# Layer 0 reordered: router ahead of the other transposes, convolution behind the expert tiles, lag terms by outer products

## The chip, the cores and the metric

The kernel runs on one core of a Trainium2 chip. All of its numbers are float32. The metric is the device time of one execution in microseconds (us). The core has five engines that run their own in-order queues side by side: PE (TensorE, matmuls and transposes, with its weight loads shown apart as PEld), DVE (VectorE), ACT (ScalarE), POOL (GpSimd) and SP (SyncE, which here only issues DMAs). POOL issues the indirect DMAs, those whose rows are found by a list of indices. Engines wait for one another by semaphores.

## The reference, cut to what matters

The program is four layers over x of 16 sequences of 256 tokens of 128 features. Only layer 0 is touched by the change:

```python
xn = layernorm(x)                                  # no scale, no shift
x  = x + L0_attn(xn) + L0_ffn(xn)

def L0_attn(x):                                    # a state space layer, 64 states for each of 128 channels
    u  = layernorm(x) * ln_gamma + ln_beta
    dt = exp(log_dt)
    dA = exp(-exp(log_A) * dt[:, None]); dB = B_param * dt[:, None]
    # for each step t:  h = dA*h + dB*u[..., None];  y[t] = einsum('dn,bdn->bd', C_param, h) + D_param*u
    return x + y @ W_out.T + b_out

def L0_ffn(x):                                     # 8 experts, the two best of each token, and a shared expert
    xn = layernorm(x) * ln_scale + ln_bias
    probs = softmax(xn @ gate_w.T);  top 2, scaled to sum to 1 -> w
    out = swiglu(x, sWg, sWu, sWd)
    for e in range(8):
        out = out + w[:, e:e+1] * swiglu(x, Wg[e], Wu[e], Wd[e])
    return out                                     # swiglu(x, g, u, d) = (silu(x@g) * (x@u)) @ d
```

The recurrence is linear, so y is a causal convolution of u along the sequence. Its weight at lag l, in channel d, is the sum over the 64 states n of C[d,n] * B[d,n] * dt[d] * exp(-exp(log_A[d,n]) * dt[d] * l), and D[d] is added at lag 0.

The other layers (attention over 16 heads and a gated network; a window of 3 and a ternary network; attention and a coupling network) follow in the same program.

## The kernel before, in words

The 4096 tokens lie in 8 blocks X[0] to X[7] of 512 tokens; a block is 128 partitions by 4 groups by 128 features. Blocks 0 to 3 are half 0, blocks 4 to 7 half 1.

`prepare(hf)` (L163) does, for one half: mean and variance of X (`stats`, L115), r = 1/std (`inv_std`, L107), xn (`normalise`, L122), its transposes xT (L173), the sum X + xn on POOL (L175), statistics of xn once more, z = xn normalised a second time, z's transposes, the router's scale and shift on DVE (rT, L186), the logits (lg, L189), and `route` (L209). `route` picks the two best experts of each token and gives each (token, expert) a slot in a list sorted by expert, in tiles of 256 slots that each belong to one expert (23 tiles a half, 46 in all). For that it counts, for every token and expert, the tokens ahead of it: within a group of 128 tokens by a product with a triangular matrix, and over the groups ahead by 15 products with a matrix of ones into the same bank (pos, L243 to L245).

`scatter` (L294) writes the rows xn to their slots in DRAM (XS), by 32 indirect DMAs a half. XS is filled with zeros first, by four DMAs from a tile of 128 x 2944 zeros (L154).

The convolution needs the lag weights. `lag_rates`, `lag_terms` and `lags_done` (L315 to L334) work them out state by state: for each of 64 states an Exp of 128 x 256 on ACT (dec) and a multiply-add on DVE into kern; kern goes to DRAM (kd). `convolved` (L196) makes u from z (gamma, beta on DVE), turns it round in time by a product with a reversed identity (ru) and puts it into U. `toeplitz(g)` (L339) loads, for four channels, 128 overlapping windows of kd as a matrix of 128 x 4 x 256 (toe, 512 KB), and `conv(g)` (L345) multiplies it with U (cv) and copies the result to Y; g runs to 32. `mixed(i)` (L439) transposes Y and adds its product with W_out and the bias to X.

The tile loop (L480 to L499) works on tile k: `fetch_weights` (the expert's weights, POOL, four tiles ahead), `fetch_slots` (256 rows xs of XS, SP, three ahead), `turn_slots` (two transposes, xsT), `up_slots` (sg, su, silu and product hs) and `down_slots` (sy, its copy ys, and a store to YS). From tile 6 on one conv(g) goes with each tile. From tile 29 on, `fetch_outputs` gathers the rows of half 0 back from YS (yk, POOL) and `combine` adds them, weighted, to X. Behind the loop follow mixed for half 0, then half 1's gathers beside mixed for half 1, then half 1's combines.

What sets the order: inside `tc.manual_schedule` (L467) each engine issues the instructions of the region in the order in which they are written. Outside it, and for how the instructions of the region fall among the others, a planner that works with costs of its own decides; of two ready instructions it takes the one that was written first. A queue doesn't overtake: an instruction that waits holds back what is behind it on its engine, SP's and POOL's DMA issues included.

## Time and profile before

| | |
|---|---|
| median of 14 runs | 1717.78 us (1710.58 to 1729.92) |
| the profiled execution: its own time | 1724.39 us |
| its span, first to last instruction | 1722.4 us |
| mean granted clock of PE | 0.909 |
| layer 0 up to the first matmul of layer 1 (pq) | 525.3 us |
| of that: first transposes of a tile (xsT) at | 210.3 us |
| last sy of the last tile ends at | 446.3 us |

The page shows for each engine a row of 40 digits: the busy tenths of 40 equal slices of the span. Rows of stages give the stretch, its length, then the busy time of PE, PEld, DVE, ACT and POOL with the number of instructions, the granted clock, the share of the DMA engines and GB/s. Rows of the timeline give start, duration, engine, line, operation, written and read tiles, how many were merged, and in brackets the idle time of the engine before it and what ended it. "issue" there means that nothing in the profile explains the wait; "remote" means a semaphore whose sender isn't seen. Rows of the chain give start, duration, engine and tile. A matmul of float32 stands as two passes, so 8 products are x16.

### The profile page before, as it was taken

To read this page: it belongs to the slowest core of one execution; us is meant where nothing else is said; L and a number is where in the kernel's file an instruction comes from. 1 tells how busy PE (TensorE), PEld (TensorE's weight loads), DVE (VectorE), ACT (ScalarE), POOL (GpSimd) and SP (SyncE) were. 2 spreads that over 40 slices of the span, in tenths; PEclk is the share of its full clock that TensorE was granted. 3 is DMA by queue.
4 is the path that set the end of the run, shared out by engine and by line. 5 is a ranking of instruction groups with operands and counts; after the bars stand their busy time and mean duration, and the time that the engine had idled before them with its cause. 6 is when DMAs were issued, how large, how long until landed. Compare 5 with 4: busy or idle time off the path is not lost.

```text
span 1722.4 us, 28078 instructions
## 1 busy us (share of the span) xinstructions
PE 1485.5 (86%) x11820; PEld 951.7 (55%) x11820; DVE 747.3 (43%) x1644; ACT 656.9 (38%) x1047; POOL 278.5 (16%) x269
## 2 busy tenths in 40 slices
PE   3646489988827999999999999999989999998998
PEld 2434378887514666666555455555545666664344
DVE  6537122222256555553344333533335655552223
ACT  2336222221104454443224333433334445435543
POOL 1442421145360000000001111111100000000222
PEclk9966799998758899998999999999998999988898
DMA  6120267785130000000000000000000000000000
GB/s 229 37 68 17 76 183 224 223 243 152 45 135 1 2 2 2 2 2 2 1 1 1 1 1 0 0 1 0 0 1 2 2 2 2 2 2 1 0 25 25
DMA packets 60142, 73.78 MB, mean 43 GB/s; under 512 B 5233, under 2 KB 53490, under 8 KB 59378
## 3 DMA queue, kind: packets, MB, share of 16 engines
q1 hardware_dynamic: 51376, 43.18, 7.8%
q0 software_dynamic: 7920, 27.08, 5.6%
q8 instruction: 94, 1.54, 0.4%
q10 hardware_dynamic: 722, 1.73, 0.3%
q14 instruction: 30, 0.25, 0.0%
HBM read 53.42 MB, written 18.55 MB: 42 GB/s over the span
## 4 chain that ended last, share of the span: by engine, by line
PE 72%; DVE 9%; ACT 7%; DMA 6%; issue 4%; another core or an unknown queue 2%; POOL 1%; SPq 0%; DVEq 0%; ACTq 0%; POOLq 0%
PE h L105 13%; PE se L105 8%; PE sc L105 7%; PE po L105 7%; PE c L105 5%; DMA xs<-XS 5%; PE av L105 4%; ACT E L688 4%; DVE M L646 3%; PE mT L661 2%; PE pq L105 2%; PE cv L105 2%; PE sg L105 2%; PE pv L105 2%
## 5 line engine op out<-in xcount | busy, mean ns | idle before, releaser
L646 DVE TENSOR_REDUCE M<-sc 128x4 f32<-128x1024 f32 (+3 forms) x256 | 196.0, 819 | 113.8 <-PE sc L105 113.8
L105 PE MATMUL h<-h,pk 128*128 128x512 f32 x512 | 221.0, 592 | 0.0
L688 ACT ACTIVATE E<-se 128x1024 f32<-128x1024 f32 (+1 forms) x192 | 158.8, 879 | 107.2 <-PE se L105 107.0
L105 PEld LDWEIGHTS h<-h,pk 128*128 128x128 f32 x512 | 97.3, 190 | 119.0 <-issue 115.3
L105 PE MATMUL sc<-Kp,Qm 32*128 32x192 f32 (+3 forms) x2048 | 136.3, 349 | 21.7 <-ACT E L688 21.5
L105 PE MATMUL se<-Q,Km 32*128 32x256 f32 (+3 forms) x2048 | 131.4, 344 | 13.2 <-DVE M L646 11.6
L105 PEld LDWEIGHTS sc<-Kp,Qm 32*128 32x128 f32 x2048 | 100.3, 198 | 70.1 <-ACT E L688 35.0
L815 POOL TENSOR_TENSOR pr<-q,k 128x512 f32<-128x512 f32 (+2 forms) x24 | 28.4, 1210 | 607.3 <-ACT k L808 429.8
L105 PEld LDWEIGHTS se<-Q,Km 32*128 32x128 f32 x2048 | 94.5, 194 | 51.9 <-issue 44.4
L939 POOL TENSOR_TENSOR xT<-xT,c 128x512 f32<-128x512 f32 x24 | 30.2, 1278 | 442.2 <-DVE c L938 442.2
L865 ACT ACTIVATE h<-h,pk 128x512 f32<-128x512 f32 x64 | 44.0, 687 | 144.3 <-PE h L105 144.2
L875 DVE TENSOR_TENSOR x<-x,po 128x512 f32<-128x512 f32 x8 | 5.5, 688 | 170.4 <-PE po L105 170.4
L133 PE MATMUL xnT<-consts,xn 128*128 128x128 f32 x128 | 28.5, 364 | 59.0 <-DVE xn L124 59.0
L412 DVE TENSOR_TENSOR hs<-hs,su 128x512 f32<-128x512 f32 x46 | 31.6, 688 | 108.7 <-PE su L105 91.3
L105 PE MATMUL av<-E,vals 128*32 128x256 f32 (+3 forms) x2048 | 78.4, 306 | 0.0
L297 POOL DMA_INDIRECT XS<-xn,slots x64 | 63.4, 991 | 63.6 <-DVE te L277 44.4
L381 POOL DMA_INDIRECT we<-in_w0e,rows x46 | 43.9, 954 | 166.5 <-PE sy L105 99.9
L105 PE MATMUL c<-c,pk 128*64 128x512 f32 (+2 forms) x144 | 70.1, 635 | 0.0
L430 POOL DMA_INDIRECT yk<-YS,slots x64 | 60.7, 949 | 33.7 <-issue 15.8
L105 PE MATMUL py<-shared,h 128*128 128x128 f32 x128 | 20.2, 311 | 53.2 <-issue 25.8
L703 ACT COPY cu<-av 128x512 f32<-128x512 f32 x32 | 18.8, 586 | 121.8 <-PE av L105 121.8
L105 PEld LDWEIGHTS cv<-U,toe 128*128 128x128 f32 x512 | 64.1, 197 | 1.9
(227 smaller groups left out, 2630.6 us busy)
## 6 DMA issues: line engine op xcount, KB each, us to landing
toe<-kd SPq DMA_DIRECT2D x32, 512.0 KB
XS<-zero SPq DMA_DIRECT2D x4, 1472.0 KB
xs<-XS SPq DMA_DIRECT2D x46, 128.0 KB
YS<-ys SPq DMA_DIRECT2D x46, 128.0 KB
pk<-in_pk SPq DMA_DIRECT2D x1, 3145.5 KB
x<-in_x SPq DMA_DIRECT2D x8, 256.0 KB
out<-x SPq DMA_DIRECT2D x8, 256.0 KB
XS<-xn,slots POOLq DMA_INDIRECT x64
```

Source lines behind the costliest of these rows:

```text
L105: nc.tensor.matmul(o, l, r, start=start, stop=stop)
L133: nc.tensor.transpose(ps[:, t * P : (t + 1) * P], src[:, t, :], ident)
L297: d = nc.gpsimd.indirect_dma_start(out=XS[hf][:, :], out_offset=at_rows(slots[hf][:, k, n : n + 1]), in_=xn[n // NT][:, n % NT, :], in_off ...
L381: nc.gpsimd.indirect_dma_start(out=w["w"].rearrange("p a b -> p (a b)"), out_offset=None, in_=w0e[:, :], in_offset=at_rows(rows_of[hf][:, ...
L412: nc.vector.tensor_tensor(h, h, pu, ALU.mult)
L430: nc.gpsimd.indirect_dma_start(out=y, out_offset=None, in_=YS[hf][:, :], in_offset=at_rows(slots[hf][:, k, n : n + 1]))
L646: nc.vector.tensor_reduce(dst, src, AX.X, ALU.max, negate=True)
L661: nc.tensor.transpose(ps[:, T, c * P : (c + 1) * P], negm[bl][:, c, T].rearrange("p g j k -> p (g j k)"), ident)
L688: nc.scalar.activation(E[:, 2 * n : 2 * n + 2, :], se[n][:, :, 0 : 2 * wide], AF.Exp, scale=ISQ)
L815: nc.gpsimd.tensor_tensor(pr[:, :, j:], q[:, :, j:], k[:, :, 0 : S - j], ALU.mult)
L865: nc.scalar.activation(hn[:, c, :], ps, AF.Gelu, scale=W2[sn][:, c : c + 1])
L939: nc.gpsimd.tensor_tensor(xT[i], xT[i], cpl, ALU.add)
```

## The change

It rewrites layer 0's order and three of its parts. Nothing behind layer 0 is touched.

- **prepare**: the second normalisation is worked out from the first one's figures (r1 and off), so z comes straight from X, on ACT, without xn and without a second round of statistics. z, the logits and `route` are written ahead of xn, its transposes and xT. rT moves from DVE to ACT, the copy of the logits from ACT to DVE, and X + xn out of it (now `add_norm`, on DVE, between tiles).
- **route**: the 15 products of ones become one, and the sum over the groups ahead becomes a scan on DVE (four doublings).
- **zeros**: one DMA a half, from a tile of 128 x 128 that is read again and again, and only after the last input has landed.
- **lag terms**: exp(rate * l) is split into exp(rate * fine) * exp(rate * coarse) with l = coarse + fine, each 16 values; the sum over states is 128 small products on PE (`lag_sums`), 64 rows by 16 columns, and eight stores to kd. `lag_rates`, `lag_terms`, `lags_done` go.
- **order**: half 0's 32 scatters and the first 15 of half 1's are written ahead of the loop; the other 17 go one at the start of each of the first 17 tiles. Between up_slots and down_slots of every second tile goes one piece of: lag_sums; then for each block add_norm, for half 1 its shared expert, and convolved. The 32 toeplitz and conv steps follow the loop, with half 1's gathers and combines between them; then mixed for all 8 blocks, then the last combines.

```diff
-        zero = wp.tile([P, TILES * SLOTS // 2], F32, tag="zero", name="zero")
+        zero = wp.tile([P, D], F32, tag="zero", name="zero")
...
-            flat = XS[hf].rearrange("(q p n) d -> q p (n d)", q=2, p=P)
-            zeroed.append([nc.sync.dma_start(out=flat[q], in_=zero) for q in range(2)])
+            flat = XS[hf].rearrange("(p n) d -> p n d", p=P)
+            zeroed.append([nc.sync.dma_start(out=flat, in_=zero.unsqueeze(1).to_broadcast([P, TILES * SLOTS // P, D]))])
+            for z in zeroed[hf]:
+                tc.add_manual_dep(z.ins, xin[-1].ins.name, sync, reason="inputs first")
...
             r = inv_std(sp, mv, N, "r0" + tag)
+            nc.vector.tensor_tensor(r1, r, r, ALU.mult)
+            nc.vector.tensor_tensor(r1, r1, mv[:, :, 1], ALU.mult)
+            nc.vector.tensor_scalar(r1, r1, EPS, None, ALU.add)
+            nc.scalar.activation(r1, r1, AF.Sqrt)
+            nc.vector.reciprocal(r1, r1)
+            nc.vector.tensor_tensor(r1, r1, r, ALU.mult)
+            nc.vector.scalar_tensor_tensor(off, mv[:, :, 0], -1.0, r1, ALU.mult, ALU.mult)
...
+                for t in range(NT):
+                    k = n * NT + t
+                    nc.scalar.activation(
+                        z[:, t, :], X[i][:, t, :], AF.Identity, bias=off[:, k : k + 1], scale=r1[:, k : k + 1]
+                    )
+                ps = transpose4(z, f"zT{i}")
+                rT = sp.tile([P, 512], F32, tag="rT", name=f"rT{i}")
+                nc.scalar.activation(rT, ps, AF.Identity, bias=W0["lnb"], scale=W0["lns"])
...
+            route(logits, hf)
             for n, i in enumerate(blocks):
                 normalise(xn[n], X[i], mv, r, n * NT)
                 ps = transpose4(xn[n], f"xnT{i}")
                 nc.scalar.copy(xT[i], ps)
-                nc.gpsimd.tensor_tensor(X[i], X[i], xn[n], ALU.add)
-                stats(sp, xn[n], mv1[:, n * NT : (n + 1) * NT, :], f"st1_{i}")
...
-            mm(pos[:, 0 : N * E], W0["upper"], flat, True, False)
-            for k in range(1, N):
-                mm(pos[:, k * E : N * E], ones2, flat[:, 0 : (N - k) * E], False, k == N - 1)
+            mm(pos[:, 0 : N * E], W0["upper"], flat)
+            mm(pos[:, N * E : 2 * N * E], ones2, flat)
...
+            while k < N:
+                V.tensor_copy(run[1][:, 0:k, :], run[0][:, 0:k, :])
+                V.tensor_tensor(run[1][:, k:N, :], run[0][:, k:N, :], run[0][:, 0 : N - k, :], ALU.add)
+                run.reverse()
+                k *= 2
...
+        def lag_sums(parts):
+            ps = [bank(f"lag{h}") for h in range(2)]
+            for k in range(16):
+                for c in range(4):
+                    for h in range(2):
+                        r = slice(64 * h, 64 * h + 64)
+                        mm(
+                            ps[h][32 * c : 32 * c + 16, 16 * k : 16 * k + 16], parts["coarse"][r, 4 * k + c, :],
+                            parts["fine"][r, 4 * k + c, :],
+                        )
+            for h in range(2):
+                for c in range(4):
+                    r = slice(32 * c, 32 * c + 16)
+                    nc.vector.tensor_copy(kt[r, h], ps[h][r, 0:256].rearrange("p (k b) -> p k b", b=16))
...
+            for h in range(2):
+                for c in range(4):
+                    dst = bass.AP(
+                        tensor=kd.tensor, offset=kd.offset + (64 * h + c) * 384 + P,
+                        ap=[[16, 16], [4 * 384, 16], [1, 16]],
+                    )
+                    nc.sync.dma_start(out=dst, in_=kt[32 * c : 32 * c + 16, h])
...
-        lag_rates()
         xn0, zs0 = prepare(0)
         for n in range(HN):
-            scatter(0, xn0, n)
+            for k in range(2):
+                scatter(0, xn0, n, k)
+        xn1, zs1 = prepare(1)
+        inside = TILES - 6
+        early = 2 * HN - inside
+        second = [(n, k) for n in range(HN) for k in range(2)]
+        for nk in second[:early]:
+            scatter(1, xn1, *nk)
         for i in HALVES[0]:
             shared_expert(i)
-        convolved(0, zs0)
-        xn1, zs1 = prepare(1)
-        for n in range(HN):
-            scatter(1, xn1, n)
-        for s in range(0, 64, 4):
-            lag_terms(range(s, s + 4))
-        lags_done()
-        for i in HALVES[1]:
-            shared_expert(i)
-        convolved(1, zs1)
+        parts = lag_weights()
...
+        between = [lambda: lag_sums(parts)]
+        for i in range(NBLK):
+            between.append(lambda i=i: add_norm(i))
+            if i in HALVES[1]:
+                between.append(lambda i=i: shared_expert(i))
+            between.append(lambda i=i: convolved(i, zs[i]))
...
             for k in range(NJ):
+                if k < inside:
+                    scatter(1, xn1, *second[early + k])
                 if k + 4 < NJ:
                     fetch_weights(k + 4)
...
-                g = k - 6
-                if 0 <= g < 32:
-                    if g + 3 < 32:
-                        toeplitz(g + 3)
-                    conv(g)
+                if between and k % 2 == 0:
+                    between.pop(0)()
                 down_slots(k)
...
+            for g in range(3):
+                toeplitz(g)
+            for g in range(32):
+                if g + 3 < 32:
+                    toeplitz(g + 3)
+                conv(g)
+                if g == 0:
+                    combine(0, HN - 1)
+                if g % 2 == 1 and g // 2 + 4 < HN:
+                    fetch_outputs(1, g // 2 + 4)
+                if g >= 6 and g % 2 == 0 and (g - 6) // 2 < HN:
+                    combine(1, (g - 6) // 2)
+            for i in range(NBLK):
                 mixed(i)
-            for n in range(5):
-                fetch_outputs(1, n)
-            for i in HALVES[1]:
-                mixed(i)
-            for n in range(HN):
-                if n + 5 < HN:
-                    fetch_outputs(1, n + 5)
+            for n in range(13, HN):
                 combine(1, n)
```

## The prediction

> **What bounds the kernel now.** I read the page, then busy time by stage, then the timeline where engines stand still. Layer 0 runs to about 525 of 1722 us and the diff touches nothing behind it. The page's slices are 43 us each:

> ```profile
> span 1722.4 us, 28078 instructions
> ...
> PE   3646489988827999999999999999989999998998
> ...
> PEclk9966799998758899998999999999998999988898
> DMA  6120267785130000000000000000000000000000
> ```

> PE is full behind layer 0 and half empty in its first five slices and in slices 11 and 12. By stage (PE, PEld, DVE, ACT, POOL, clock, DMA):

> ```profile
> 60.00:106.00 46.00, 17.70 (x57) 9.85 (x56) 13.20 (x52) 7.56 (x10) 35.72 (x36) 0.73 0.18 59
> 155.00:210.00 55.00, 30.05 (x103) 16.98 (x102) 20.84 (x45) 23.18 (x39) 32.15 (x32) 0.74 0.24 73
> 240.00:411.00 171.00, 157.81 (x1076) 146.31 (x1075) 38.85 (x75) 40.51 (x127) 46.38 (x49) 0.95 0.74 217
> 446.00:525.00 79.00, 36.70 (x147) 23.80 (x145) 39.39 (x152) 10.29 (x18) 37.25 (x41) 0.59 0.26 87
> ```

> While POOL scatters (rows one, two) nothing else is busy; while convolution rides on the tiles (row three) PE is the bound. The timeline shows why the tiles start late:

> ```profile
> 61.96 1.00 POOL L297 DMA_INDIRECT XS<-xn,slots  x1 [0.30 <-DVE st L119]
> ...
> 98.87 0.69 DVE L372 TENSOR_TENSOR x<-x,py 128x512 f32<-128x512 f32 x1 [22.51 <-issue]
> ...
> 104.34 2.13 SPq L389 DMA_DIRECT2D xs<-XS  x3
> ...
> 155.78 1.01 POOL L297 DMA_INDIRECT XS<-xn,slots  x1 [44.41 <-DVE te L277]
> ...
> 201.59 1.08 ACT L365 ACTIVATE h<-pg 128x512 f32<-128x512 f32 x2 [25.36 <-remote]
> ...
> 210.27 0.60 PE L399 MATMUL xsT<-consts,xs 128*128 128x128 f32 x4
> ```

> Half 0's slots are fetched at 104, yet the first tile is turned at 210: half 1's router, its shared experts and the lag terms stand before it. In both bursts of scatters PE's results reach DVE and ACT some 20 us late (98.87, 201.59). The trace doesn't tell why; I call it the hand-over stall.

> So three stages: to the first tile 210.3; tiles to 446.3 (end of the last sy), 236; tail to the first pq of layer 1 (525.3), 79.

> **Router first.** Half 0's r stands at 12.9. The second normaliser is now worked out from it: five small DVE steps, a square root and a reciprocal (0.15 to 0.25 each with hops), +1.9. z moves to ACT, 16 times 128x128: between the 0.30 of the 128x128 Exp (L222) and the 0.51 of the 128x256 dec (L329); I take 0.35 (its size is the former's), 1.4 a block. Blocks ran 3.7 apart (lg 1.88, zT 1.0, rT 0.81 in turn); I leave that, since PE's in-order alternation sets it. Logits at 15 + 1.4 + 4 x 3.7 = 31, not 40.3: -9. Removing the second statistics costs nothing to anyone.
> In the route 30 passes of pos go (6.4 us, 52.65 to 59.06). The scan adds 11 DVE steps at some 0.25, 2.5; the small steps from tot to te (52.3 to 56.2), covered by pos until now, stand open for some 2. Net -2; and z's gamma and beta, which sat between the steps (41.5 to 43.9), are gone: -2. First scatter at 62 - 13 = 49. If xn's first block, moved behind the route, is not squeezed into gaps: +1.2.

> **Scatters.** POOL's pitch is 1.275 (0.97 and 0.30). 32 take 41, to 90; 15 of half 1, 19, to 109, provided its route is done by 90: its logits follow 15 after half 0's, and its route of some 15 follows half 0's, so 68. First weights: issue 1.0 and about 3 to land, 113. I add 5 for the stall: first turn at 118, **-92**. PE must fit transposes (10) and half 0's shared experts (29 now, in 59 to 76 and 106 to 118) into 49 to 113; less a stall of 23 that leaves 41, just enough. Ends: 100, if weights go ahead of scatters (one did, at 60.50); 140, if both hand-overs of half 1's route (tot, pos) wait out 21 each on PE.
> Costed at nothing, with its cover:
> - The zeros wait for the last input now and go in 512-byte pieces (packets of that size took 28.5 ns each on SP's queue in this trace): 11,776 pieces on 16 engines, 21 us, half 0's done near 27 against scatters at 49; if they are later, the scatters are late by as much. Queued behind them on SP are only the xs fetches, at 90.
> - lag_weights: two Exp and four products over 128x1024 elements, at the 0.88 of the page's 128x1024 Exp (L688) and twice the 0.68 of a 128x512 product about 8 us on two engines that were 16 to 29% busy in 60 to 106. They replace 64 dec and 64 kern steps (30.0 us on ACT, 30.8 on DVE), which stood in the stages to 175. If the cover fails, lag_sums waits, and with it tile 0.
> - The logits' copy changes engine (0.19, 8 of them), and xn's addition moves from POOL (1.27) to DVE (0.69), there beside PE's sy.
> - The second square root: its table is the one just loaded; if ACT puts Exp between, 1.28 each time.

> **Tiles.** Without convolution the tiles were bound by xs: sy began at 218.44, 223.93, 227.24, 232.01, 235.12, 4.17 a tile, alternately with and without a wait, although PE needs only 3.5. An extra PE step in every second tile therefore adds in full: a pair takes 8.35, and with an extra (3.5 + extra) + 4.85. 29 tiles x 4.17 + 17 with gathers x 4.35 (411 to 446) = 195. Extras:
> - lag sums: 128 products of 64 rows by 16 columns, two passes each, 256. Nearest above is cv, 0.106 a pass (16 in 1.69); nearest in shape is av with 32 columns:

> ```profile
> 240.25 1.69 PE cv L105 x16
> 563.68 2.31 PE av L105 x64
> ```

> So 0.036 to 0.106, 9 to 27 us; I take 0.045, 11.5, as it is nearer to av. Behind it SP waits: eight copies and an add on DVE (3.2), eight stores at 0.42 (3.4), then YS(0) and xs(4), 6 more. 17 in all, 13 to 35.
> - convolved, eight times: in DVE's queue gamma and beta wait behind hs, PE's ru waits for them and sy(k) queues behind ru: 0.2 + 0.6 + 0.64 + 0.68 + 0.1 + 0.96 = 3.2; 25.6.
> - half 1's shared experts, four times: pg, pu 3.44, wait for h 1.0, py 1.75: 6.2; 24.8.
> - add_norm ahead of ys: 2.
> 195 + 69 = 264, **+28**. Ends +15 (waits hide some) and +60. POOL's scatter per tile (1.27) and weights (1.27) fit into 4.2; weights are fetched four tiles ahead.

> [...]

> The stores of the lag terms are 2048 pieces of 64 bytes. [...] At the 512-byte price they take 3.6 us, and their reader comes some 250 us later, so even several times that is free.

> **Tail.** Convolution now stands alone. toe(0) is issued behind the last YS: ys 0.6, two issues 0.8, landing 4.4:

> ```profile
> 328.40 4.37 DMA toe<-kd
> ```

> Together 5.8 of idle PE. Then 32 steps: PE 1.75 (1.69 to 1.85); DMA 32 pieces of 1 KB per engine at 49.7 ns, 1.6, and one gather, 0.23; buffers (4.85 + 1.75)/4 = 1.65. Close together, so 2.0: 64. Ends 1.8 and, at the 217 GB/s of row three for 512 + 64 KB, 2.7: 58 to 86. Half 1's gathers, which filled 482 to 506, lie beside it; the first wait on POOL for the last YS to land, with only later gathers queued behind, and DVE asks for them six steps on. Eight mixed blocks at the undisturbed pitch 2.57 (446.79, 449.37, 451.94), 20.6, and 1.0; before they took 33. Six combines, 2.1. Then to pq: 14.5 before (510.8 to 525.3); half 0's norm can now run beside mixed, 11. Sum 104.5, **+25.5** (+18 to +48).

> **Sum.** -92 + 28 + 25.5 = -38.5. The profiled execution took 1724.39 (span 1722.4 and 2.0 around it), 6.6 above the median 1717.78. It becomes 1686; on the median's scale 1679, I say 1680.

> **Rivals.**
> - Slower: the stall enters the tile loop. For: among seven gathers back to back (from 425.8) xsT ended at 430.39 and was copied at 436.58, 6.2 late; now POOL issues DMAs in all 46 tiles. Against: with one weight fetch a tile (217 to 360) none is seen. It decides from six stalls (38.5/6.2); in every fifth tile, nine: 56, 1736.
> - Transfers bound the convolution (2.7 each): +22, 1702. For: the DMA share is 0.74 already; against: that was PE-bound.
> - Late start at 140: +22, 1702. For: the stall lasted to the 30th scatter both times. With the one above: 1724.
> - The change doesn't act: PE keeps half 1 ahead of the tiles, start near 175: -35 + 53.5, 1736. Against: what stood there is moved in the source into the ordered region.
> - More gain: start 100, extras half hidden: 1650.

> **Chances.** Forecast 0.45 (1662 to 1700); stall in the loop or no effect 0.17; transfers 0.12; late start 0.10; both 0.08 (about no change); more gain 0.08. A difference under 0.3% (5 us) can't be told from none. Faster 0.75, same 0.08, slower 0.17. The range leaves out the far slower cases and the best: 1645 to 1727.

> **What would show it.** First scatter near 49, not 62; first xsT at 100 to 140; lag passes at 0.036 to 0.106; tile pairs of 8.3 without extras; cv steps 2.0 apart with PE, not DMA, ahead of them; PE slices 2 to 4 fuller. I am wrong if xsT is copied long after its transposes within the loop, or if toe is what cv waits for.

## The result, and the profile after

The changed kernel takes 1795.86 us (median of 10 runs, 1787.94 to 1805.65) against 1721.53 for the kernel before (47 runs): a ratio of 1.0426, with a 95% interval of 1.0400 to 1.0452. The forecast was 1680 us, and its range went up to 1727. So the sign is wrong, and the range did not hold the time.

The profiled execution has a span of 1785.3 us, 62.9 more than before. The first product of layer 1 (pq) starts at 591.7 us where it started at 525.3, and what lies behind it is 3.5 us shorter (1193.6 after 1197.1). So all of the loss is in layer 0. The page of the changed kernel, its 40 slices (45 us each; the digits are tenths):

```profile
span 1785.3 us, 28284 instructions
...
PE   2456777764996799999999999999998999998999
...
PEclk9678898995556899999899999999998999988888
DMA  7123444533532000000000000000000000000000
```

In slices 10 to 12 (400 to 540 us) the granted clock stands at 5 tenths, and in slices 11 and 12 PE is nevertheless full. That stretch is the convolution, which now stands alone behind the tiles. By stretches (us of the stretch; then busy PE, PEld, DVE, ACT, POOL, each with its instructions; granted clock, DMA share, GB/s):

```profile
75.00:100.00 25.00, 1.55 (x4) 0.38 (x2) 4.41 (x20) 3.65 (x6) 15.17 (x16) 0.59 0.20 63
131.00:400.00 269.00, 191.45 (x1193) 156.03 (x1192) 87.83 (x170) 56.77 (x114) 85.58 (x89) 0.90 0.43 117
414.00:444.00 30.00, 3.65 (x16) 4.08 (x16) 5.65 (x16) 0.33 (x2) 18.94 (x20) 0.50 0.23 64
444.00:537.00 93.00, 93.00 (x436) 93.00 (x437) 0.00 (x0) 9.38 (x58) 0.00 (x0) 0.50 0.46 147
538.00:566.00 28.00, 28.00 (x112) 17.52 (x110) 4.81 (x7) 4.68 (x8) 0.00 (x0) 0.72 0.00 0
566.00:592.00 26.00, 8.22 (x33) 5.82 (x33) 21.08 (x113) 5.81 (x10) 6.82 (x9) 0.61 0.43 174
```

Row one is the hand-over stall among the scatters, as before. Row four decides: 93 us in which PE is busy without a gap at half the clock, 436 passes of 0.214 us. Row three is a second loss: 30 us with 16 passes while POOL's gathers run. The chain that ended last says the same (start, us, what):

```profile
117.00 8.56 another core or an unknown queue
...
396.63 4.27 DMA toe<-kd
401.04 13.20 PE cv L105 x61
...
431.56 2.60 issue
...
443.97 93.42 PE cv L105 x437
537.68 1.12 PE YT L133 x4
...
573.01 6.40 DMA pk1i<-in_pk1i
...
591.70 1.14 PE pq L105 x2
```

One toe is waited for, the first (4.27); behind 443.97 none is. A pass of cv took 0.106 us before (16 in 1.69) and takes 0.214 here (93.42 by 437).

The lag sums, ahead of the first tile's sy, are short (from the timeline, 256 passes in all):

```profile
134.69 1.96 PE L105 MATMUL lag<-lag_fine,lag_coarse 64*16 64x16 f32 x216
138.86 0.49 PE L105 MATMUL lag<-lag_fine,lag_coarse 64*16 64x16 f32 x40 [2.22 <-issue]
```

By the three stages of the forecast:

| | forecast | measured |
|---|---|---|
| first xsT | 118 | 127.5 |
| tiles, to the end of the last sy | 264 | 268.3 (127.5 to 395.75) |
| from there to the first cv | 5.8 | 5.3 |
| 32 convolution steps | 64 | 136.6 (401.0 to 537.7) |
| eight mixed blocks | 21.6 | 28.3 |
| combines, norm and the rest to pq | 13.1 | 25.7 (566.0 to 591.7) |
| pq | 486.5 | 591.7 |

### The profile page after: what moved, and what is told of

Read it like the earlier page. It is cut to its first block, busy times and chain, and to the rows that moved or that the text cites. A ratio compares the mean times of both kernels' runs of the same rounds, so it can differ in the third digit from the quotient of the medians.

```text
span 1785.3 us, 28284 instructions
## 1 busy us (share of the span) xinstructions
PE 1527.7 (86%) x12020; PEld 997.0 (56%) x12020; DVE 714.8 (40%) x1534; ACT 629.0 (35%) x1002; POOL 265.2 (15%) x261
## 4 chain that ended last, share of the span: by engine, by line
PE 74%; DVE 8%; DMA 5%; ACT 5%; issue 4%; another core or an unknown queue 1%; SPq 0%; POOL 0%; DVEq 0%; ACTq 0%; POOLq 0%
PE h L105 12%; PE se L105 7%; PE po L105 7%; PE sc L105 7%; PE cv L105 6%; PE c L105 5%; PE av L105 4%; DMA xs<-XS 4%; ACT E L745 4%; DVE M L703 3%; PE mT L718 2%; PE pq L105 2%; PE tw L105 2%; PE sg L105 2%; PE pv L105 2%
## 5 line engine op out<-in xcount | busy, mean ns | idle before, releaser
L105 PE MATMUL h<-h,pk 128*128 128x512 f32 x512 | 221.0, 592 | 0.0
L105 PEld LDWEIGHTS h<-h,pk 128*128 128x128 f32 x512 | 97.3, 190 | 119.0 <-issue 115.3
L105 PE MATMUL sc<-Kp,Qm 32*128 32x192 f32 (+3 forms) x2048 | 135.9, 348 | 22.0 <-ACT E L745 21.8
L105 PE MATMUL se<-Q,Km 32*128 32x256 f32 (+3 forms) x2048 | 130.1, 341 | 13.3 <-DVE M L703 11.8
L105 PEld LDWEIGHTS sc<-Kp,Qm 32*128 32x128 f32 x2048 | 100.0, 197 | 70.7 <-ACT E L745 35.8
L105 PE MATMUL cv<-U,toe 128*128 128x32 f32 (+1 forms) x512 | 110.0, 384 | 31.7 <-issue 26.4
L105 PEld LDWEIGHTS cv<-U,toe 128*128 128x128 f32 x512 | 110.3, 332 | 31.4 <-issue 31.4
L105 PEld LDWEIGHTS se<-Q,Km 32*128 32x128 f32 x2048 | 93.5, 192 | 52.0 <-issue 44.6
L872 POOL TENSOR_TENSOR pr<-q,k 128x512 f32<-128x512 f32 (+2 forms) x24 | 28.3, 1204 | 608.5 <-ACT k L865 431.0
L996 POOL TENSOR_TENSOR xT<-xT,c 128x512 f32<-128x512 f32 x24 | 30.2, 1280 | 442.5 <-DVE c L995 442.4
L105 PE MATMUL av<-E,vals 128*32 128x256 f32 (+3 forms) x2048 | 78.4, 306 | 0.0
L105 PE MATMUL c<-c,pk 128*64 128x512 f32 (+2 forms) x144 | 70.0, 635 | 0.0
L316 POOL DMA_INDIRECT XS<-xn,slots x64 | 61.8, 965 | 24.8 <-issue 18.9
L446 ACT COPY xsT<-xsT 128x256 f32<-128x256 f32 x46 | 17.1, 372 | 135.5 <-PE xsT L444 103.0
L105 PEld LDWEIGHTS av<-E,vals 128*32 128x32 f32 x2048 | 53.1, 111 | 20.4 <-issue 2.5
```

Of the source, the lines that this page charges most:

```text
L105: nc.tensor.matmul(o, l, r, start=start, stop=stop)
L316: d = nc.gpsimd.indirect_dma_start(out=XS[hf][:, :], out_offset=at_rows(slots[hf][:, k, n : n + 1]), in_=xn[n // NT][:, n % NT, :], in_off ...
L446: nc.scalar.copy(v["xT"], ps[:, 0:SLOTS])
L872: nc.gpsimd.tensor_tensor(pr[:, :, j:], q[:, :, j:], k[:, :, 0 : S - j], ALU.mult)
L996: nc.gpsimd.tensor_tensor(xT[i], xT[i], cpl, ALU.add)
```

## The experiments

The runs of the experiments fell on five chips, of two kinds. On one, here called chip A, the kernel before takes 1716 us, near the 1722 of the runs of the result, whose chip is not on record. On the other four it takes 1643 to 1651; they are all called chip B here (one in each of the first, third, fourth and fifth round). Most of the difference is one thing: on chip B the hand-over stall is missing (shown below). So every kernel is given as a ratio to the kernel before on its own chip.

### First round, chip B: is it the clock, and what sets the clock?

The first change paces half 1's gathers, so that the row of gathers is not mixed up with the clock:

```diff
-            for h in range(2):
-                nc.scalar.copy(
+            for h, copy in enumerate((nc.scalar.copy, nc.vector.tensor_copy)):
+                copy(
                     Y[:, h::2, 4 * g : 4 * g + 4],
...
-                y = fetched[hf, n, k] = sp.tile([P, D], F32, tag="yk", name=f"yk{hf}_{n}_{k}", bufs=12)
+                y = fetched[hf, n, k] = sp.tile([P, D], F32, tag="yk", name=f"yk{hf}_{n}_{k}", bufs=6)
```

> The changed kernel, with one of the two copies of each convolution step moved from ACT to DVE (ahead of the combines in DVE's queue) and 6 instead of 12 buffers for gathered rows, so that half 1's gathers keep step with the convolution instead of running back to back from 399 to 439. Burst theory (the row of software DMAs holds up every engine's signals): the one-instruction-every-0.7-us stretch from 414 to 444 goes, the convolution takes 32 x 3.42 = 109 us of solid PE instead of 137, time near 1768 (1760 to 1778). Rival (the toe transfers or their four buffers hold PE in that stretch): the stretch stays, 1796. By both the granted clock stays at 0.50 in the convolution.

Measured: ratio 1.0513 (1.0477 to 1.0548). The convolution is solid, from 369.7 to 478.9 us, 109 us as expected, at half the clock:

```profile
370.00:478.00 108.00, 108.00 (x508) 108.00 (x508) 15.51 (x59) 6.58 (x31) 27.42 (x31) 0.50 0.53 167
75.00:100.00 25.00, 21.87 (x98) 14.43 (x97) 7.98 (x12) 5.51 (x10) 18.90 (x21) 0.93 0.23 73
```

The second row is the surprise. While POOL scatters as densely as ever (18.90 of 25 us), PE is busy for 21.87 us, where it had 1.55 in the profile after. This chip has no hand-over stall, and so the run says nothing on what causes it. The clock it does show: PE has no gap, and a pass still takes 0.21 (108.00 by 508).

The second kernel is the one with paced gathers, and adds a product of 512 columns to each step, into a bank that nobody reads:

```diff
+        def filler(g):
+            mm(bank(f"fill{g}"), ident, shared.rearrange("p a b -> p (a b)")[:, 0:512])
...
                 conv(g)
+                if g >= 0:
+                    filler(g)
```

> The kernel with paced gathers, and in every convolution step one more product: identity by 512 columns of the shared weights into a bank that nobody reads (0.86 us at the full clock, by the changed kernel's pg rows at 72.95 to 73.81). Work is only added. Clock theory (the granted clock follows how many columns stream through PE, and 16- and 32-column passes alone do not raise it): the clock goes to 0.9 or more, a step takes 16 x 0.106 + 0.86 = 2.56 us, the convolution 82 us, 28 less than with paced gathers alone: near 1741. Rival (the clock is halved here for another reason, or a pass takes 0.21 us for another reason than the clock): a step takes 3.42 + 0.86 to 1.72, 4.3 to 5.1 us: 28 to 55 us more, 1796 to 1823.

Measured: 1.0835 (1.0792 to 1.0878), 51 us more than with paced gathers alone. The clock did not rise:

```profile
363.00:525.00 162.00, 161.92 (x574) 129.93 (x574) 15.51 (x59) 6.58 (x31) 28.60 (x31) 0.50 0.36 113
```

The third has it in the first 12 steps only:

```diff
                 conv(g)
+                if g < 12:
+                    filler(g)
```

> As the one before, but the added product stands only in the first 12 of the 32 steps. If the clock must be fed all the time: 12 x 2.56 + 20 x 3.42 = 99 us, near 1758, and the granted clock falls back to 0.50 within one or two records (3.4 us each) of the 12th step. If it only has to be raised once and dense passes then keep it: 12 x 2.56 + 20 x 1.70 = 65 us, near 1724. If the added product does nothing for the clock: 12 x 4.3 to 5.1 + 20 x 3.42, 120 to 130 us, 1779 to 1789.

Measured: 1.0623 (1.0588 to 1.0658), 17 us more than with paced gathers; the convolution takes 130 us, and the clock is 0.50 throughout. In this form my clock theory had fallen: some wide products are not enough.

The fourth kernel is the kernel before with one part of the change alone, the place of the convolution:

```diff
-                g = k - 6
-                if 0 <= g < 32:
-                    if g + 3 < 32:
-                        toeplitz(g + 3)
-                    conv(g)
...
+            for g in range(32):
+                if g + 3 < 32:
+                    toeplitz(g + 3)
+                conv(g)
             for i in HALVES[0]:
                 mixed(i)
```

> The kernel before, with nothing changed but the place of the convolution: its 32 steps stand behind the 46 tiles, ahead of the first mixed block. Clock theory: the tile loop shrinks from 236 to 195 us, and the convolution alone takes 5.8 + 32 x 3.42 = 115 us at a granted clock of 0.50: 1722 - 41 + 115 = 1796, as slow as the whole change. Rival (the convolution behind the tiles is as fast as beside them, and something else of the change slows it): 5.8 + 32 x 1.75 to 2.0, 62 to 70 us, 1743 to 1751.

Measured: 1.0542 (1.0507 to 1.0578), where 1796 of 1722 is 1.043. This one move, 91 us on its chip (1735.8 after 1644.9), costs as much as the whole change did. No gathers go beside the convolution here. The tiles shrink to 207 us (155.5 to 362), and the convolution takes 106 (361.9 to 468) instead of riding along:

```profile
75.00:100.00 25.00, 19.89 (x108) 15.05 (x107) 17.35 (x39) 17.25 (x35) 19.21 (x20) 0.84 0.16 51
156.00:362.00 206.00, 158.63 (x827) 139.63 (x827) 59.30 (x119) 45.10 (x94) 75.65 (x80) 0.88 0.52 147
363.00:468.00 105.00, 104.98 (x503) 104.87 (x502) 0.75 (x3) 10.14 (x62) 11.33 (x12) 0.51 0.49 154
```

Its front is that of the kernel before, and there too the stretch of 75 to 100 us is full of work on this chip (19.89 of PE; 5.07 on chip A). Its first tile is turned at 155.5 instead of 210.3. That is 55 of the 77 us by which this chip is faster; where the other 22 lie is not shown, as no profile of the kernel before was taken on it.

**The second clock theory.** A clock record lasts 3.41 us in these traces. I summed the columns of all passes that start within each record ahead of the first pq (each float32 product makes two passes) in the six traces so far, and looked at the clock of the record that follows. After 1280 columns or fewer, it was at full speed in 0 of 374 cases; after 1792 or more, in 436 of 447; between them in 17 of 54. What fits is a count of columns, not busy time (PE was busy for 93.00 of 93 us at 0.50 in the profile after), and the bounds are much the same at both speeds: after 1792 to 2047 columns the full clock followed in 20 of 22 records at full speed and in 20 of 25 at half. The rule was made from these traces; the runs that follow test it. In their ten traces the counts are 0 of 444, 754 of 773, and 51 of 111 between. A convolution step streams 16 passes of 24 columns on average, 384. Alone, that is 383 a record at half the clock (3.42 us a step) and would be an estimated 770 at the full one (16 passes of 0.106): both lie where no record that followed was at full speed. Beside a tile (512 + 1024 + 1024 + 1024 columns for xsT, sg, su, sy) it is an estimated 2500, and the granted clock there was 0.95 in the profile before. And one added product makes 1408 a step: 940 a record at half the clock (5.1 us a step, clock 0.50 throughout), by this count too few to rise, but an estimated 1850 at the full one (some 2.6 us a step), enough to stay.

### Second round, chip A: the second theory, and the convolution put back

So the added products need a start: eight of them between the last tile and the first step, ahead of one in each step as in the second kernel of the first round.

```diff
             for g in range(3):
                 toeplitz(g)
+            for j in range(8):
+                filler(-j)
             for g in range(32):
```

> The changed kernel itself, as it is, beside the others, since the kernel before took 1645 us on the chip of the first four runs and 1722 on the chip of the records. If that chip lacks the hand-over stall (in the run with paced gathers no engine was held up between 71 and 98): first tile turned near 96 instead of 128, and on such a chip the convolution keeps clear of the stall too, so pacing the gathers wins nothing there: ratio near 1.05, as with paced gathers. If the gathers stall it on that chip too: 28 us more than with paced gathers, ratio 1.068.

Measured: chip A, 1.0458 (1.0414 to 1.0502), with both stalls; the profile after repeated.

> Paced gathers, eight of the added 512-column products between the last tile and the first convolution step (while the first toe lands), and then one in every step. New clock theory, from the records of six traces (layer 0): the clock of a 3.4-us record is 1.0 when about 1800 or more columns streamed in the record before it, whatever its speed, and 0.5 when fewer than about 1400 did. At 0.50 a step with one added product streams 384 + 1024 columns in 5.1 us, 940 a record, so it can never rise (which the run with one added product showed); at the full clock the same step takes 2.56 us, 1880 a record, and stays up once it is up. So: clock 1.0 through the convolution, 32 x 2.56 = 82 us, 27 less than with paced gathers alone although work is added (1702 on a chip where that took 1728). Rival (the clock is halved in the convolution for another reason): 5.1 us a step, 163 us, as in the run with one added product (1780 on that chip).

Measured: 1.0090 (1.0058 to 1.0121), 1731.5 us beside 1791.6 for the changed kernel in the same round. The convolution runs from 414.5 to 498.8, 84 us, at the full clock:

```profile
415.00:498.00 83.00, 83.00 (x570) 68.18 (x568) 15.53 (x59) 6.59 (x31) 26.41 (x29) 1.00 0.67 214
```

The kernel does 40 products more that nobody needs, and it is 60 us faster than the changed kernel. The two profiled executions are 45 us apart (1787.1 and 1741.6): the convolution is 52 us shorter (136 to 84) and the mixed blocks, which now start at the full clock, 5 (26 to 21), while the first tile came 8 later (129.7 and 138.0). The paced gathers are in this too: in the changed kernel the row of gathers took 27 of the 52. The clock's part is the other 25 (109, as with paced gathers on chip B, to 84). The same 512-column product cost 51 us without the start.

The third kernel of the round is that one with `if g < 12:` ahead of the added product in the steps.

> As the one before, with the added product in the first 12 steps only. The column theory: 12 steps of 2.56 us at 1.0, then one record of 768 columns, after which the clock falls to 0.50: 20 steps of 3.42. 99 us in all, 10 less than with paced gathers alone. Rival (once raised, dense passes of any width hold it): 12 x 2.56 + 20 x 1.70 = 65 us, 44 less.

Measured: 1.0207 (1.0172 to 1.0241). The convolution takes 97 us (406.9 to 504.3; forecast 99), and the clock falls as soon as the added products end: the record from 438.8 has 704 columns and is at the full clock, the one from 442.2 is at half:

```profile
407.00:439.00 32.00, 32.00 (x218) 26.08 (x217) 5.14 (x20) 2.55 (x12) 9.01 (x10) 1.00 0.73 238
439.00:442.00 3.00, 3.00 (x29) 2.94 (x27) 0.77 (x3) 0.21 (x1) 0.05 (x1) 1.00 0.71 201
...
446.00:504.00 58.00, 58.00 (x274) 58.00 (x273) 9.33 (x35) 3.62 (x17) 16.72 (x18) 0.50 0.47 147
```

In the second row the convolution runs alone at the full clock, 29 passes in 3 us, 0.10 each: the price that I had forecast. In the last it is 0.21 (274 in 58). Once raised is not enough; the rival is out. In the first two rows PE did not wait for the toe transfers either, at 201 to 238 GB/s. The second is shorter than two steps, though, so whether the transfers would keep up with 32 bare steps at the full clock, as the forecast had it, is not shown.

The fourth kernel keeps the change's front and takes its tail back:

```diff
-        between = [lambda: lag_sums(parts)]
-        for i in range(NBLK):
-            between.append(lambda i=i: add_norm(i))
-            if i in HALVES[1]:
-                between.append(lambda i=i: shared_expert(i))
-            between.append(lambda i=i: convolved(i, zs[i]))
+        at(0, lag_sums, parts)
+        for i in range(NBLK):
+            at(1 + i, across_z, i, zs[i])
+            at(2 + i, reversed_z, i, zs[i])
+            at(12 + 2 * i, add_norm, i)
+        for n, i in enumerate(HALVES[1]):
+            at(2 + 2 * n, shared_up, i)
+            at(3 + 2 * n, shared_down, i)
+        for g in range(32):
+            at(7 + g, toeplitz, g)
+            at(10 + g, conv, g)
...
+                for f, a in between.pop(k, ()):
+                    f(*a)
                 down_slots(k)
```

`across_z` is gamma and beta on DVE, `reversed_z` the product ru and its copies to U; `shared_up` and `shared_down` are the two halves of `shared_expert`. Behind the loop stand mixed, the gathers and the combines as in the kernel before.

> The change with the convolution put back beside the tiles: new router, lag terms by outer products and scatters between tiles as in the change; the eight convolved blocks in tiles 1 to 9 (their DVE steps one tile ahead of their PE step), half 1's shared experts in tiles 2 to 9 (up in one tile, down in the next), one convolution step in each of the tiles 10 to 41, and then the end of the kernel before. Tiles: 14 x 4.17 + 32 x 5.3 + lag sums 7 + 8 x 0.9 + 4 x 5.2 = 264 us; start 96 to 131 by the chip; then 79 as in the kernel before. If the clock theory holds, the convolution is cheap there (0.106 a pass) and the time is 0.97 of the kernel before where the stall is, and 0.995 (0.975 to 1.015) where it is not. Rival (what made the change slow is not the place of the convolution): 1.03 or more.

Measured: 0.9732 (0.9680 to 0.9784), 1666.7 us: faster than both kernels. First xsT at 127.1, last sy near 385, pq at 463.5: 258 us of tiles (forecast 264) and 78.5 of tail (forecast 79). The convolution's passes beside the tiles, and then the stretch by engines, clock and DMA:

```profile
L105 PE MATMUL cv<-U,toe x512: 192/263/276, 205.2 to 367.9; 128*128 128x16 f32 x86, 128*128 128x32 f32 x85
```

```profile
205.00:369.00 164.00, 153.28 (x1081) 142.80 (x1080) 46.11 (x91) 40.34 (x125) 61.01 (x65) 0.98 0.77 234
```

(The three numbers of cv are the shortest, the median and the longest record in ns; in the profile after they are 182, 374 and 419.) The first tile comes 83 us earlier than in the profile before (127.1 and 210.3), where the prediction had 92. So the change loses by its tail. This run takes back the order of the gathers, mixed blocks and combines too; that the place of the convolution alone is enough to lose as much was shown in the first round.

### Third to fifth round: the hand-over stall

On chip A the stall takes 25 us of the front and 27 of the convolution. What it looks like in the convolution of the profile after (PE's matmuls; the bracket is PE's idle time before each):

```profile
425.77 0.21 PE L105 MATMUL cv<-U,toe 128*128 128x32 f32 x1 [2.58 <-issue]
428.57 0.18 PE L105 MATMUL cv<-U,toe 128*128 128x16 f32 x1 [2.59 <-issue]
431.38 0.19 PE L105 MATMUL cv<-U,toe 128*128 128x16 f32 x1 [2.63 <-issue]
```

They stand 2.80 apart, four times 0.70; with the weight loads between them (424.37, 427.17, 429.98) one instruction every 1.40, and near the end of the stretch a pair every 0.70. ACT is held up too (0.33 us of work in these 30 us), and in the front DVE (waits of 2.5 to 3.3 us between small steps of the route, from 79 to 96). PE runs freely again from 444, 5 us behind the last gather (438.7).

A first attempt is the version with the new front and the convolution beside the tiles, in which every ninth scatter is to wait until the one before it has landed:

```diff
+GROUP = 8
...
+            if scatters[hf] and len(scatters[hf]) % GROUP == 0:
+                tc.add_manual_dep(d.ins, scatters[hf][-1].ins.name, sync, reason="group before landed")
```

> The version with the new front and the convolution beside the tiles, with one more wait: every ninth scatter waits until the one before it has landed, so that at most 8 go back to back. Backlog theory of the hand-over stall (some 16 software DMAs in a row fill something that all engines' signals pass through, at 0.7 us each): on a chip with the stall, half 1's route ends near 80 instead of 97, PE's shared experts run between 75 and 105 without the gap of 25 us, and the first tile is turned near 106 to 112 instead of 127, although the scatters themselves end some 9 us later: 15 to 20 us less, ratio 0.962 where 0.973 was. Rival (the stall comes from the number of scatters or from something else on that chip, not from their following one another closely): the gap stays, the scatters' delay adds, 0.973 to 0.98. On a chip without the stall: 0.99 to 1.0, and nothing learned of the gap.

Measured: chip B, 0.9798 (0.9745 to 0.9851). The scatters kept their pitch of 1.27 us without a break (the wait didn't act), so this is the version with the new front once more, on the other chip: there too it beats the kernel before.

> The changed kernel with paced gathers once more, since its first run fell on a chip without the stall. On a chip with the stall, beside the changed kernel's 1.046: burst theory 28 us less, ratio 1.03 (1.025 to 1.034), the convolution in 109 us without the one-instruction-every-0.7-us stretch. Rival (that stretch is the toe transfers): 1.046, 137 us. On a chip without the stall: 1.05 again.

Measured: chip B, 1.0490 (1.0430 to 1.0551), convolution 109 us.

The next version puts four additions of 128x512 on POOL after every eighth scatter ahead of the tiles:

```diff
+        scratch = wp.tile([P, 512], F32, tag="scratch", name="scratch")
+        nc.gpsimd.memset(scratch, 0.0)
+        pause = []
...
+            if pause:
+                tc.add_manual_dep(d.ins, pause.pop().ins.name, after, reason="pause first")
             scatters[hf].append(d)
+            if len(scatters[hf]) % 8 == 0 and len(scatters[1]) < 15:
+                for _ in range(4):
+                    w = nc.gpsimd.tensor_tensor(scratch, scratch, scratch, ALU.add)
+                    tc.add_manual_dep(w.ins, d.ins.name, after, reason="pause behind the group")
+                pause.append(w)
```

> In the run before this, the wait of every ninth scatter did not act: the scatters kept their pitch of 1.27 us. Here POOL works out four additions of 128x512 (some 1.3 us each) among every eight scatters ahead of the tiles, so that they come 1.9 us apart on average; otherwise the version with the new front and the convolution beside the tiles. Half 0's scatters end 15 us later, near 108, half 1's early ones near 137. Backlog theory of the hand-over stall: on a chip with the stall, half 1's route ends by 82 instead of 97, the shared experts run between 75 and 105 without a gap of 25 us, and the time is 0.96 to 0.975 of the kernel before. Rival (the stall does not depend on how close the scatters follow): the gap stays, 0.975 to 0.985. On a chip without the stall nothing is learned of the gap; there the pauses cost 5 to 15 us (0.985 to 0.99).

Measured: chip B, 0.9911 (0.9883 to 0.9939). No stall without the pauses, none with them; the first xsT comes at 106.5 instead of 95.1, and the ratio is 0.011 higher.

> The changed kernel with paced gathers, since both runs of it fell on a chip without the stall. On a chip with the stall: burst theory 28 us less than the changed kernel's 1.046, near 1.03, convolution in 109 us; rival (toe transfers): 1.046, 137 us. On a chip without the stall: 1.05.

> The changed kernel with paced gathers, asked again because the three runs of it fell on chips without the hand-over stall. On a chip with the stall: burst theory, 28 us less than the changed kernel's 1.046, near 1.03, convolution in 109 us; rival (the toe transfers): 1.046, 137 us.

> The version with pauses among the scatters, asked again for the same reason. On a chip with the stall: burst theory, no gap of 25 us between 71 and 98, half 1's route ended by 82, 0.96 to 0.975 of the kernel before; rival (the stall does not depend on how close the scatters follow): the gap stays, 0.975 to 0.985.

All three fell on chip B: 1.0518 (1.0492 to 1.0544) and 1.0495 (1.0437 to 1.0553) for the paced gathers, 0.9898 (0.9849 to 0.9948) for the pauses. They repeat the numbers above and tell nothing of the stall. So the theory that the stall comes from scatters that follow one another closely was not tested on a chip that has it.

What can be said of it: on chip A, in the second round, the changed kernel made 23 cv passes between 414 and 444 us at 66 GB/s:

```profile
414.00:444.00 30.00, 4.48 (x23) 5.54 (x23) 6.00 (x17) 0.33 (x2) 20.22 (x22) 0.50 0.23 66
```

The two kernels with paced gathers had no such gap there (570 passes of PE in 83 us at 214 GB/s). So the toe transfers alone don't make it. Pacing came with half of the Y copies on DVE, so whether it was the pitch of the gathers alone was not separated, and why one chip has the stall and another hasn't stays open. So does whether signals queue somewhere, and where.

## Why the prediction was wrong, point by point

- **Router first**: right in kind. The blocks kept their pitch of 3.7 (lg at 20.53, 24.23, 27.92, 31.61), the logits stood at 33.5 (forecast 31), the first scatter began at 52.1 (49). Two weight fetches went ahead of it.
- **Scatters, first turn**: forecast 118, measured 127.5, inside its ends of 100 and 140. The term that was too tight is "less a stall of 23 that leaves 41, just enough": a second stall, the 8.56 us at 117.00 in the chain, was not in it. The first one also held up half 1's route: its first scatter came at 97.9, where the sum had it follow at 90 without a gap (POOL stood for 5.57 us). On a chip without the stall the front brings the first tile to 95.6 (before: 155.5).
- **Lag sums**: all 256 passes were done in 4.7 us, where the sum had 11.5 and at least 9. They took 0.009 to 0.012 each, and 2.22 us between them is not explained by the profile. My 0.045 is four to five times too high, and the lower end of my range, 0.036, did not hold it either. The nearest row in shape (av with 32 columns) was still far from 16 columns of 64 rows. The wait behind it was of the kind that was forecast: the next xs was issued at 147.65, behind the stores of the lag terms, and PE stood for 7.26 us ahead of the transposes at 150.53. Together some 12 us, for 17. The 64-byte pieces, which no run had shown, took 10.4 ns each on SP's queue (2048 packets; those of 512 bytes 28.2).
- **Tiles**: 264 forecast, 268.3 measured. The chain alternates between xs (3.5 to 4.6 us each) and the extra step of every second tile, as in the pair model. Part of the agreement is luck: the lag sums cost 5 less than forecast, and without the convolution the tiles of the kernel before took 206 us (on chip B) where the sum had 195.
- **Tail**: the step that failed is "Then 32 steps: PE 1.75 (1.69 to 1.85) ... Close together, so 2.0: 64. Ends 1.8 and ... 2.7". PE's price was read where the convolution ran beside tiles, at a granted clock of 0.95, and carried to a place where it runs alone. There a step costs 3.42, because the clock is 0.50, and the upper end, 2.7, came from transfers, which PE waited for only once, at the start. That is 45.4 us of the 72.6 by which the convolution missed (109.4 instead of 64). The other 27 are the row of gathers, which I had put beside it at no cost.
- **The rest of the tail**: mixed started at half the clock (28.3 for 21.6). And "half 0's norm can now run beside mixed, 11" did not happen: POOL's fills for layer 1 and the load of pk1i start only when the last mixed block has ended at 566 (573.01 in the chain), 25.7 for 13.1.
- **Rivals**: none of them was it. The stall in the tile loop that I feared is small (6.4 us at 383). It came in the convolution instead, where I had not priced it. Transfers did not bound the convolution at the clock that it had (PE was busy for 93.00 of the 93 us from 444, at 0.50).
- **Two slips in reading**, which no term rests on: counted from one, the later slices in which PE is half empty are the 12th and 13th (digits 2 and 7), not the 11th and 12th; and that nothing else is busy while POOL scatters is too strong, as PE has 17.70 us of work in the 46 of row one.

Of the 105 us between forecast and measurement at pq, 45 are the clock in the convolution, 27 the gathers in it, 19 the rest of the tail, 14 the start and the tiles. Without the first two, by this sum, pq would stand near 519, some 6 us ahead of the kernel before: the front's gain and the moved work would about cancel.

## What to carry to other kernels

A duration taken from a trace holds for the clock of its place: here a pass of cv took 0.106 us beside the tiles, at a granted clock of 0.95, and 0.214 alone, at 0.50. Before a run of narrow products is moved out from among wide ones, count the columns that will stream in 3.41 us, one clock record, without them. After 1280 or fewer (of float32, both passes counted) none of 818 records here was at full speed, and the convolution's passes took twice as long, however full PE was (93.00 of 93 us); between 1280 and 1792 it went either way (68 of 165). And work that looks free beside a busy engine can be what keeps that engine's clock up: with eight added products ahead of the convolution and one in each step it ran at 1.00, and in the run where they ended with the 12th step the clock was 0.50 for the last 58 us.
